# A planned four-block transformer kernel: first loads reordered, small vector operations counted as sharing GpSimd's way, urgencies chosen anew

## The chip, the cores and the metric

The kernel runs on one core of one Trainium2 chip. The metric is the device time of one execution in microseconds, as the median of several runs. The engines are named as the profile names them: PE multiplies matrices, PEld loads its weights, DVE is the vector engine, ACT the scalar engine, POOL is GpSimd, and SP issues most of the loads.

## The reference

Eight sequences of 128 tokens, 256 features wide, pass through four blocks in float32. Each block attends over the same context (also 8 x 128 x 256) and has an MLP with 1024 hidden features.

```python
x = L0(x, ctx)     # layer norm; 16-head cross attention, boolean key mask; gelu MLP
x = L1(ctx, x)     # the latents attend over [context; latents], interleaved k/v weights, integer key mask; RMS norm; MLP
x = L2(x, ctx)     # two cross attentions, 16 heads of 128 features (2048 wide), one learned key and value each; MLP with exact gelu
x = L3(x, ctx)     # self attention with a given score mask, cross attention with another, tanh-gelu MLP
```

Every attention is `softmax(q k^T * scale, masked) v`, followed by an output product and the residual. The time goes into the wide attentions of L2, where q, k and v are 256 by 2048 products.

## The kernel before

The eight sequences are cut into five threads of 1, 1, 2, 2 and 2 sequences (`SIZES`). A thread runs all blocks in order, and the threads overlap: at most three are in the front blocks at once, three in the wide attentions (`FRONTS`, `WIDES`). The last thread's last block is split by sequence (`BY_BATCH`), and some keys and values of L2 are made ahead of time (`AHEAD`).

No order is written by hand. Each piece of work is a Python generator that asks for an operation on an engine. The class `Plan` runs these generators against a planned clock: when an engine is free in the plan, `_choose` takes the asked operation with the lowest urgency; asking for an activation table that is not loaded adds 2.5 to it on ACT. The operation is then issued, so that the instruction order of every engine is what the plan decided. Operations written as `either(...)` go to whichever of ACT and DVE comes to them first. The urgencies are the numbers in `U` (by kind of work) and `LATE` (added for each thread and stage).

How long an operation takes in the plan comes from `_weight`, which also says whether a DVE operation shares its way to SBUF with POOL. If it does, `_end` starts it in the plan at POOL's end, and lets POOL start only after it. In the version before, DVE operations on at most eight elements per partition are never shared:

```python
if n <= 8:
    return 68 + 55 * max(0, len(aps) - 2) * (name == "tensor_scalar"), False
```

A norm's reciprocal square root (`root`) is one planned operation made of ten such small instructions on tiles `rv`, `ry`, `rz`. `dma` plans when a load lands, from a running end `dma_until`; a load marked `early` may also be issued from ACT's queue. If PE has nothing to do in the plan and its planned clock would fall, `idle_work` puts in a filler, a matmul `ident` by `ident` whose result nobody reads. Two PSUM banks serve products (`mm`), two serve transposes and small results (`tl`), four serve scores (`sc`).

All operations pass through one helper, `Engine.call`, and so stand under one line, L335, in the profile. They are told apart by their tiles: `mm<-hT,w` is a projection, `tl<-ident,t` a transpose of softmax weights, `kb<-mm` an eviction, `t<-sc,mask` a masked score, `mx` and `sm` a maximum and a sum of the softmax. In the instruction orders each tile has a number of its own.

Of the kernel before, what the change touches and what calls it, by code (L numbers as in the profile page):

```python
# [18 lines left out]
P = 128  # L19
# [43 lines left out]
FRONTS, WIDES = 3, 3  # L63
BY_BATCH = (4,)
AHEAD = [[(1, 0), (1, 1)], [], [(1, 0)], [], []]
U = {'take': 0.75, 'taken': -1, 'norm': 1.33, 'mask': 5.29, 'k': 2.24, 'q': 0.77, 'v': 3.01, 'by key': 0.17, 'softmax': 1.71, 'weights': 1.17, 'pairs': 0.21, 'out': 0.57, 'mlp norm': -0.18, 'mlp 1': 2.92, 'mlp 2': 3.41, 'wide norm': 1.02, 'wide k': 3.4, 'wide q': 3.13, 'wide v': 5.44, 'wide s': 4.05, 'wide': 0.43, 'ahead': 3.67, 'load': -0.56, 'early': 0.98}
LATE = [(4.59, -1, -1, -0.66, 1.03, -1, 2.77, 3.05, 3.1, 3.0, 2.25, 1.84, 0.92), (16.8, 0.32, 4.0, 6.02, 1.18, -1, 3.37, 3.57, 8.14, 4.15, -0.94, 0.09, 0.94), (2.67, 10.11, 4.03, 1.81, 2.31, 3.16, 3.3, 3.73, 4.79, 13.74, 3.59, 9.93, 9.83), (4.81, 12.33, 4.01, -1, -0.06, 1.37, 3.1, -0.03, 1.5, 1.56, 0.96, -0.5, -1), (1.56, 2.64, -0.58, -0.46, 1.42, -0.16, 4.41, 1.29, 0.75, -1, -1, 3.81, -0.53)]


class Event:  # L70
# [14 lines left out]
class Plan:  # L85
# [12 lines left out]
    def __init__(self):  # L98
        self.now = 0
        self.seq = 0  # L100
        self.events = []
        self.asked = []
        self.until = {e: 0 for e in self.SEEN}
        self.weight, self.shared, self.wrote = 0, False, []
        self.idle_work = None
        self.both_until = {"DVE": 0, "POOL": 0}
        self.clock = Clock()
        self.count = 0
        self.log = []
        self.table = None  # L110
        self.dma_until = 2500
        self.live = {}

    def spawn(self, gen, urgency, after=0):
        end = Event()
        self.live[id(gen)] = gen
        self._later(self.now + after, (gen, urgency, end), None)
        return end
# [146 lines left out]
def _weight(eng, name, args, kw):  # L265

    aps = [x for x in (*args, *kw.values()) if isinstance(x, bass.AP)]
    sizes = [x.free_size() for x in aps]
    n = max(sizes)
    if name == "dma_start":  # L270
        return 480, False
    by_part = sum(m == 1 for m in sizes[1:]) if n > 2 else max(0, len(aps) - 2) if name == "tensor_scalar" else 0
    on_sbuf = all(x.space == bass.MemoryType.SB for x in aps)
    if eng == "PE":
        if name == "transpose":
            return 109, False
        lhsT = kw["lhsT"]
        cols = aps[0].free_size()
        if lhsT.shape[0] < P:
            return 0.539 * cols, False  # L280
        if lhsT.free_size() < P:
            return 0.494 * cols, False
        return max(225, 1.7 * cols), False
    if eng == "ACT":
        if "accum_out" in kw:
            return 385, False
        if name == "copy":
            return 61 + 0.824 * n, False
        return 127 + 0.805 * n + (35 if on_sbuf and n == 256 else 0) + (40 if isinstance(kw.get("bias"), bass.AP) else 0) + (
            90 if isinstance(kw.get("scale"), bass.AP) else 0), False  # L290
    if eng == "DVE":
        if name == "tensor_scalar" and n == 4 and len(aps) == 2 and len(args) > 5:
            return 145, False
        if name == "reciprocal":
            return 65 + 6.25 * n, False
        if name in ("bn_stats", "bn_aggr"):
            return (330 if name == "bn_stats" else 150), False
        if n <= 8:
            return 68 + 55 * max(0, len(aps) - 2) * (name == "tensor_scalar"), False
        if name in ("tensor_scalar", "tensor_copy") and on_sbuf:  # L300
            return 75 + 0.8 * n + 55 * by_part, True
        two = name in ("tensor_tensor", "scalar_tensor_tensor") and sum(
            x.space == bass.MemoryType.SB and x.free_size() > 1 for x in aps[1:]) == 2
        return 72 + 1.03 * n + 55 * by_part, two
    if name == "memset":
        return 20 + n, False
    if n <= 16:
        return 195 + 75 * by_part, False
    if name == "tensor_tensor":
        inner = any(x.ap[-1][0] == 0 for x in aps[1:])  # L310
        return 100 + (1.85 if inner else 2.3) * n, False
    return (150 + 3.0 * n, 10 + 3.6 * n, 5 * n - 20)[by_part], False
# [44 lines left out]
def four_blocks(ctx: ExitStack, tc: tile.TileContext, a: dict, out: bass.AP):  # L357
# [5 lines left out]
    plan = Plan()  # L363
# [73 lines left out]
    def dma(f, kb_, early):  # L437

        def sync():
            f(nc.sync)  # L440
            plan.weight += max(0, plan.dma_until - plan.now - 3500)

        yield op("SP", sync) + (op("ACT", lambda: f(nc.scalar)) if early else ())
        plan.dma_until = max(plan.dma_until, plan.now) + kb_ * 2.8
        yield plan.dma_until - plan.now + 2300

    def load(dst, src, kb_, early=False):
# [189 lines left out]
    def norm(T, src, e, w, b, adds, rows, hT, ready, row_done, urgency):  # L637
# [4 lines left out]
        else:  # L642
# [48 lines left out]
                    nc.vector.tensor_scalar(xn[:, i, :], src[:, i, :], y[:, i, :], z[:, i, :], ALU.mult, ALU.add)  # L691

            yield from each(*(either(lambda i=i: scaled_act(i), lambda i=i: scaled_dve(i)) for i in range(nb)))
        spawn(add_rows(adds, rows, row_done, nb), urgency)
        yield (tl, 1)
        pt = bank("tl")[:, : NC * T.nt].rearrange("p (c b k) -> p c b k", c=NC, b=nb)

# [3 lines left out]
                    nc.tensor.transpose(pt[:, c, i, :], xn[:, i, c * P : (c + 1) * P], ident)  # L701

        yield op("PE", transposes)

        def out_act(c):
            to, s = hT[:, c, :], pt[:, c].rearrange("p b k -> p (b k)")
# [21 lines left out]
    def add_rows(adds, rows, row_done, nb):  # L728
        for (dst, src, _), (r, e) in zip(adds, rows):
            yield e  # L730
            yield op("POOL", lambda: nc.gpsimd.tensor_tensor(
                dst, src, r.unsqueeze(1).to_broadcast([P, nb, D]), ALU.add))
            plan.put(row_slots)
        plan.set(row_done)
# [73 lines left out]
    def key_bias(mask, dst, hs, ks, ks_in, name, dtype, T, may_be_none):  # L808

        nb = T.nb
        raw = mask[:, 0].bitcast(dtype)[:, :, :P]
        m = mask[:, 1]
        ms = new(act, [P, 2, nb], "ms", bufs=4)
        kss = new(act, [P, 2, NC, nb], "kss", bufs=4)
        yield spawn(load(raw, a[name][:, T.tokens].rearrange("o (b k) -> o b k", k=P).partition_broadcast(P), 64 * nb), -1)
        some = new(act, [P, nb], "some", bufs=4)

        def minus():
            nc.vector.tensor_scalar(m, raw, 0.0, -BIG, ALU.is_equal, ALU.mult)
            if may_be_none:
                nc.vector.tensor_reduce(some, m, AX.X, ALU.max)
                nc.vector.tensor_scalar(some, some, -1.0, None, ALU.is_ge)
            else:
                nc.vector.memset(some, 1.0)
            for e in range(2):
                nc.vector.tensor_scalar(hs[:, e], some, half[e], None, ALU.mult)
                nc.vector.tensor_scalar(ms[:, e], some, mask_row[e], None, ALU.mult)  # L830

        def biases():
            for e in range(2):
                for c in range(NC):
                    nc.vector.tensor_scalar(kss[:, e, c], some, ks[:, e, c : c + 1], None, ALU.mult)

        yield op("DVE", minus)
        yield ks_in
        yield op("DVE", biases)
        yield from each(*(  # L840
            op("ACT", lambda e=e, c=c, b=b: nc.scalar.activation(
                dst[:, e, c, b, 0, :], m[:, b], AF.Identity, bias=kss[:, e, c, b : b + 1], scale=ms[:, e, b : b + 1]))
            + op("POOL", lambda e=e, c=c, b=b: nc.gpsimd.tensor_scalar(
                dst[:, e, c, b, 0, :], m[:, b], ms[:, e, b : b + 1], kss[:, e, c, b : b + 1], ALU.mult, ALU.add))
            for e in range(2) for c in range(NC) for b in range(nb)))
# [646 lines left out]
    def inputs():  # L1492
        for T in threads:
            h = T.h
            early = h < 2
            rows = (load(T.x, a["x"][T.batches].rearrange("b p d -> p b d"), 128 * T.nb, early),
                    load(T.ctx, a["ctxT"].rearrange("(c p) t -> p c t", p=P)[:, :, T.tokens], 128 * T.nb, early))
            for f, then in zip(rows, (T.ready, ctx_in[h])):
                spawn(all_then([spawn(f, -3)], then), 0)
            if h == 0:  # L1500
                spawn(all_then([spawn(load(cols, a["cols"], 140, True), -3)], cols_in), 0)
                first = new(const, [P, 1], "first")
                spawn(asks(op("ACT", lambda: nc.scalar.activation(first, ident[:, :1], AF.Exp), None, EXP)), 9)
            spawn(blocks(T), 0)
            yield 4000 if h == 0 else 8000
# [46 lines left out]
```

## Time and profile before

| what | value |
|---|---|
| median of 3 runs | 1195.21 us (1195.16 to 1196.08) |
| the profiled execution | 1194.78 us |
| its span | 1193.0 us |
| mean granted PE clock | 0.993 of full |
| busy: PE, PEld, DVE, ACT, POOL | 1150.5, 956.5, 798.8, 596.3, 360.4 us |
| loaded from HBM | 178.5 MB |

The span runs from the first to the last instruction; the execution has 1.8 us around it. A float32 matmul appears as two PE records, a transpose as one. Their ends are modelled, so PE's busy time is not the time that it needs; the distance from one start to the next shows its pace.

### The profile page before, as it was taken

The page shows a single profiled execution, that of the slowest core. Times are in us where ns is not written, and L with a number is a line of the kernel's source. Part 1 is how long each engine was busy: PE and PEld are TensorE (multiplying, and loading weights), DVE is VectorE, ACT ScalarE, POOL GpSimd, SP SyncE. Part 2 cuts the span into 40 slices and gives each one's busy share as a digit, 9 for nine tenths or more (in the row PEclk, how much of TensorE's full clock was granted, in tenths as well). Part 3 has the DMA queues.
Part 4 walks back from the last instruction along what each step waited for, and adds up shares of the span by engine and source line. Part 5 has one row for each costly group of instructions (what it writes and reads, how often), then busy time and mean ns, then how long its engine had stood idle before and what let it go on. Part 6 is the DMA issues. An engine that isn't in the chain of part 4 may idle for free.

```text
span 1193.0 us, 23579 instructions
## 1 busy us (share of the span) xinstructions
PE 1150.5 (96%) x8816; PEld 956.5 (80%) x8816; DVE 798.8 (67%) x2186; ACT 596.3 (50%) x1538; POOL 360.4 (30%) x446
## 2 busy tenths in 40 slices
PE   7999999999999999999999999999999999988978
PEld 6677788888888878887887878888787778877767
DVE  6867568747776586787477265556855657678972
ACT  3555455355445374557353343633553336367872
POOL 2211211223124253013202022412532226165770
PEclk8999999999999999999999999999999999998999
DMA  9754567787645554435334534446443564351120
GB/s 299 219 162 136 160 201 214 238 273 229 190 143 196 152 185 145 135 112 147 117 116 141 165 106 145 124 131 187 138 137 122 139 183 133 117 143 55 32 85 19
DMA packets 134706, 181.09 MB, mean 152 GB/s; under 512 B 8896, under 2 KB 83392, under 8 KB 134592
## 3 DMA queue, kind: packets, MB, share of 16 engines
q1 hardware_dynamic: 133344, 178.55, 48.7%
q8 instruction: 70, 1.15, 0.4%
q10 hardware_dynamic: 1248, 1.03, 0.3%
q14 instruction: 44, 0.36, 0.1%
HBM read 178.50 MB, written 1.05 MB: 151 GB/s over the span
## 4 chain that ended last, share of the span: by engine, by line
PE 79%; DVE 11%; ACT 5%; DMA 2%; issue 1%; POOL 0%; SPq 0%; ACTq 0%; POOLq 0%; DVEq 0%
PE mm L335 57%; PE tl L335 17%; PE sc L335 5%; DVE rz L335 2%; ACT kb L335 1%; DVE t L335 1%; DMA w<-in_L_wk 1%; DMA bb<-in_L_bias_v 1%; ACT t L335 1%; DVE mn L335 1%; ACT q L335 1%; DVE ry L335 1%; ACT pt L335 1%; DVE kb L335 1%; DVE q L335 1%
## 5 line engine op out<-in xcount | busy, mean ns | idle before, releaser
L335 PE MATMUL mm<-hT,w 128*128 128x256 f32 (+1 forms) x1576 | 292.4, 335 | 12.0 <-ACT kb L335 2.5
L335 PEld LDWEIGHTS mm<-hT,w 128*128 128x128 f32 x1576 | 242.8, 191 | 43.5 <-issue 8.0
L335 POOL TENSOR_TENSOR t<-t,sm 128x512 f32<-128x512 f32 x128 | 132.0, 1041 | 298.5 <-DVE sm L335 242.8
L335 PE MATMUL mm<-ctxT,w 128*128 128x256 f32 (+1 forms) x768 | 148.7, 342 | 1.7 <-DVE x L335 0.8
L335 PE MATMUL mm<-w,ctxT 128*128 128x512 f32 (+1 forms) x352 | 145.9, 542 | 4.6 <-DMA w<-in_L_v_w 2.0
L335 PEld LDWEIGHTS mm<-ctxT,w 128*128 128x128 f32 x768 | 121.7, 194 | 16.5 <-issue 3.0
L335 PE MATMUL mm<-w,at 128*128 128x256 f32 x512 | 121.5, 380 | 0.2 <-DVE kb L335 0.2
L335 PE MATMUL mm<-w,kb 128*128 128x256 f32 x512 | 119.6, 382 | 0.9 <-PE mm L335 0.8
L335 POOL TENSOR_TENSOR x<-x,row 128x256 f32<-128x256 f32 (+1 forms) x48 | 48.0, 999 | 232.7 <-ACT xn L335 108.3
L335 PEld LDWEIGHTS mm<-w,at 128*128 128x128 f32 x512 | 94.7, 190 | 16.2 <-issue 2.6
L335 ACT ACTIVATE t<-t,mn 128x128 f32<-128x128 f32 x256 | 99.5, 395 | 12.8 <-DVE mn L335 11.6
L335 PEld LDWEIGHTS mm<-w,kb 128*128 128x128 f32 x512 | 94.1, 190 | 14.6 <-PE mm L335 1.4
L335 DVE TENSOR_TENSOR x<-mm,x 128x256 f32<-128x256 f32 (+1 forms) x102 | 47.6, 466 | 82.8 <-PE mm L335 82.1
L335 POOL TENSOR_TENSOR t<-t,mask 128x512 f32<-128x512 f32 x64 | 80.2, 1276 | 63.9 <-DVE t L335 62.5
L335 PEld LDWEIGHTS mm<-w,ctxT 128*128 128x128 f32 x352 | 63.0, 192 | 42.7 <-issue 33.6
L335 POOL TENSOR_TENSOR bv<-bv,bb 128x512 f32<-128x512 f32 x40 | 50.8, 1271 | 153.2 <-DMA bb<-in_L_bias_v 137.0
L335 ACT ACT_TABLE_LOAD x60 | 77.0, 1283 | 15.5 <-PE sc L335 6.7
L335 ACT ACTIVATE at<-tl,cols 128x128 f32<-128x128 f32 x212 | 60.4, 371 | 46.5 <-PE tl L335 46.2
L335 PE MATMUL tl<-ident,t 128*128 128x128 f32 x512 | 75.5, 276 | 7.7 <-ACT pt L335 4.4
L335 ACT ACTIVATE kb<-mm,cols 128x256 f32<-128x256 f32 (+1 forms) x168 | 59.5, 422 | 43.5 <-PE mm L335 43.2
L335 PEld LDWEIGHTS tl<-ident,t 128*128 128x128 f32 x512 | 60.0, 141 | 26.0 <-issue 11.6
L335 ACT ACTIVATE t<-t 128x516 f32<-128x516 f32 x64 | 40.4, 634 | 78.4 <-DVE t L335 78.4
(124 smaller groups left out, 1851.7 us busy)
## 6 DMA issues: line engine op xcount, KB each, us to landing
w<-in_L_wk SPq DMA_DIRECT2D x40, 512.0 KB, 4.7
w<-in_L_wv SPq DMA_DIRECT2D x40, 512.0 KB, 4.1
w<-in_L_wq SPq DMA_DIRECT2D x40, 512.0 KB, 4.5
w<-in_L_wo SPq DMA_DIRECT2D x40, 512.0 KB, 4.5
bv<-in_L_bv SPq DMA_DIRECT2D x40, 256.0 KB, 4.7
bb<-in_L_bias_v SPq DMA_DIRECT2D x40, 256.0 KB, 5.7
w<-in_L_mlp_w SPq DMA_DIRECT2D x20, 512.0 KB, 4.8
w<-in_L_w_fc SPq DMA_DIRECT2D x20, 512.0 KB, 4.4
```

The costliest lines, as they stand in the source:

```text
L335: return f(*args, **kw)
```

## The change

It does five things. In the order of the diff: the urgencies in `U` and `LATE` have new values, and the planned end of the first loads is 3300 instead of 2500 ns. Small DVE operations whose operands all lie in SBUF count as shared with POOL in the plan. A load's planned time per KB is 2.9 instead of 2.8 ns. Where a norm is only a transpose (`w is None`), the residual's bias rows are added after the transposes instead of before. And among the first loads the key masks of the first two threads may go over ACT's queue and are more urgent than anything but the bias columns (`cols`), which share their urgency; `x` and the context follow.

```diff
-U = {'take': 0.75, 'taken': -1, 'norm': 1.33, 'mask': 5.29, ..., 'mlp norm': -0.18, ..., 'wide norm': 1.02, ..., 'load': -0.56, 'early': 0.98}
+U = {'take': 0.15, 'taken': -0.55, 'norm': 1.33, 'mask': 5.71, ..., 'mlp norm': -1, ..., 'wide norm': 0.2, ..., 'load': 0.2, 'early': 1.82}
-LATE = [(4.59, -1, -1, -0.66, 1.03, ...
+LATE = [(4.8, 1.85, -1, 2.6, 0.57, ...
...
-        self.dma_until = 2500
+        self.dma_until = 3300
...
         if n <= 8:
-            return 68 + 55 * max(0, len(aps) - 2) * (name == "tensor_scalar"), False
+            return 68 + 55 * max(0, len(aps) - 2) * (name == "tensor_scalar"), on_sbuf and name != "memset"
...
-        plan.dma_until = max(plan.dma_until, plan.now) + kb_ * 2.8
+        plan.dma_until = max(plan.dma_until, plan.now) + kb_ * 2.9
...
-        spawn(add_rows(adds, rows, row_done, nb), urgency)
+        if w is not None:
+            spawn(add_rows(adds, rows, row_done, nb), urgency)
...
         yield op("PE", transposes)
+        if w is None:
+            spawn(add_rows(adds, rows, row_done, nb), urgency)
...
-        yield spawn(load(raw, a[name][:, T.tokens]..., 64 * nb), -1)
+        yield spawn(load(raw, a[name][:, T.tokens]..., 64 * nb, T.h < 2), -5 if T.h < 2 else -1)
...
-                spawn(all_then([spawn(f, -3)], then), 0)
+                spawn(all_then([spawn(f, -4 if early else -3)], then), 0)
...
-                spawn(all_then([spawn(load(cols, a["cols"], 140, True), -3)], cols_in), 0)
+                spawn(all_then([spawn(load(cols, a["cols"], 140, True), -5)], cols_in), 0)
```

More of the change, by code (lines that the diff above doesn't have):

```diff
@@ L65 @@
 AHEAD = [[(1, 0), (1, 1)], [], [(1, 0)], [], []]
-U = {'take': 0.75, 'taken': -1, 'norm': 1.33, 'mask': 5.29, 'k': 2.24, 'q': 0.77, 'v': 3.01, 'by key': 0.17, 'softmax': 1.71, 'weights': 1.17, 'pairs': 0.21, 'out': 0.57, 'mlp norm': -0.18, 'mlp 1': 2.92, 'mlp 2': 3.41, 'wide norm': 1.02, 'wide k': 3.4, 'wide q': 3.13, 'wide v': 5.44, 'wide s': 4.05, 'wide': 0.43, 'ahead': 3.67, 'load': -0.56, 'early': 0.98}
-LATE = [(4.59, -1, -1, -0.66, 1.03, -1, 2.77, 3.05, 3.1, 3.0, 2.25, 1.84, 0.92), (16.8, 0.32, 4.0, 6.02, 1.18, -1, 3.37, 3.57, 8.14, 4.15, -0.94, 0.09, 0.94), (2.67, 10.11, 4.03, 1.81, 2.31, 3.16, 3.3, 3.73, 4.79, 13.74, 3.59, 9.93, 9.83), (4.81, 12.33, 4.01, -1, -0.06, 1.37, 3.1, -0.03, 1.5, 1.56, 0.96, -0.5, -1), (1.56, 2.64, -0.58, -0.46, 1.42, -0.16, 4.41, 1.29, 0.75, -1, -1, 3.81, -0.53)]
+U = {'take': 0.15, 'taken': -0.55, 'norm': 1.33, 'mask': 5.71, 'k': 2.24, 'q': 0.51, 'v': 3.01, 'by key': 0.17, 'softmax': 1.71, 'weights': 1.17, 'pairs': 0.21, 'out': 0.57, 'mlp norm': -1, 'mlp 1': 2.92, 'mlp 2': 3.41, 'wide norm': 0.2, 'wide k': 3.4, 'wide q': 3.13, 'wide v': 5.44, 'wide s': 4.05, 'wide': 0.6, 'ahead': 3.42, 'load': 0.2, 'early': 1.82}
+LATE = [(4.8, 1.85, -1, 2.6, 0.57, -0.78, 2.77, 3.05, 3.1, 4.26, 0.92, 1.84, 0.92), (16.51, 0.4, 2.46, 6.11, 1.1, -1, 4.59, 3.57, 7.89, 3.63, -0.44, -1, -1), (2.67, 13.1, 4.03, 1.89, 2.39, 4.21, 4.35, 3.73, 4.79, 13.55, 3.59, 12.53, 12.43), (4.81, 10.83, 3.75, 0.32, -0.11, 1.32, 3.1, -0.03, 1.86, 1.75, 2.89, -1, 0.1), (2.69, 2.78, -0.58, -0.46, 1.42, -0.16, 3.55, 2.84, -0.29, -1, -1, 3.81, 0.54)]
 class Event:
@@ L817, in key_bias @@
         kss = new(act, [P, 2, NC, nb], "kss", bufs=4)
-        yield spawn(load(raw, a[name][:, T.tokens].rearrange("o (b k) -> o b k", k=P).partition_broadcast(P), 64 * nb), -1)
+        yield spawn(load(raw, a[name][:, T.tokens].rearrange("o (b k) -> o b k", k=P).partition_broadcast(P), 64 * nb, T.h < 2), -5 if T.h < 2 else -1)
         some = new(act, [P, nb], "some", bufs=4)
```

## The prediction

> **What bounds the kernel now.** I read the page first: span, busy times, granted clock, chain of waits.
>
> ```profile
> span 1193.0 us, 23579 instructions
> PE 1150.5 (96%) x8816; PEld 956.5 (80%) x8816; DVE 798.8 (67%) x2186; ACT 596.3 (50%) x1538; POOL 360.4 (30%) x446
> ...
> PEclk8999999999999999999999999999999999998999
> ...
> PE 79%; DVE 11%; ACT 5%; DMA 2%; issue 1%; POOL 0%; SPq 0%; ACTq 0%; POOLq 0%; DVEq 0%
> ```
>
> PE is busy 96% and carries 79% of the chain, so the time is PE work plus the places where PE runs thin. Busy is not peak, so I set a pace: in the timeline's PE rows 24 matmuls of 256 columns take 1046.90 - 1041.72 = 5.18 us, 0.216 us each.
>
> ```profile
> 1041.72 5.34 PE L335 MATMUL mm<-hT,w 128*128 128x256 f32 x24
> 1046.90 0.60 PE L335 MATMUL tl<-ident,xn 128*128 128x128 f32 x4
> ```
>
> The closest spacings of the other forms are 0.43 (512 columns), 0.111 (128) and 0.034 us (four-row-block forms). Records times spacing, fillers left out, give 1097.3 us of PE work; 1193.0 - 1097.3 = 95.7 us are lost. Placed by time: 34.9 us in 0 to 150, 27.4 in 150 to 1050, 33.4 in 1050 to 1193. The busy times of those stretches say which engine is near its limit:
>
> ```profile
> 0.00:150.00 150.00, 134.23 (x1290) 110.39 (x1291) 104.87 (x344) 71.30 (x141) 34.22 (x73) 0.97 0.63 195
> 150.00:1050.00 900.00, 891.35 (x6421) 741.86 (x6421) 591.92 (x1560) 431.25 (x1052) 243.76 (x286) 1.00 0.52 159
> 1050.00:1193.00 143.00, 124.88 (x1109) 104.25 (x1107) 101.99 (x283) 93.75 (x346) 82.37 (x87) 0.98 0.21 61
> ```
>
> Columns: PE, PEld, DVE, ACT, POOL. The long middle is PE at 99% and can hardly get better; a reordering wins or loses at the two ends. The tail's worst stall in the timeline, all engines:
>
> ```profile
> 1071.69 1.27 POOL L335 TENSOR_TENSOR t<-t,mask 128x512 f32<-128x512 f32 x1
> 1071.75 1.22 DVE L335 TENSOR_TENSOR rz<-ry 128x1 f32<-128x1 f32 x1
> ...
> 1072.91 2.04 POOL L335 TENSOR_TENSOR t<-t,sm 128x512 f32<-128x512 f32 x2
> ...
> 1073.01 0.96 DVE L335 TENSOR_TENSOR rz<-rz,rv 128x1 f32<-128x1 f32 x1
> ...
> 1074.01 0.96 DVE L335 SCALAR_TENSOR_TENSOR ry<-rz,ry 128x1 f32<-128x1 f32 x1
> ...
> 1075.91 0.69 DVE L335 COPY pt<-tl 128x512 f32<-128x512 f32 x1
> ...
> 1076.66 0.58 PE L335 MATMUL tl<-ident 128*128 128x128 f32 x1 [3.94 <-DVE pt L335]
> ```
>
> Three one-element DVE steps of a root, 0.16 us elsewhere, take 1.22, 0.96 and 0.96 and end with the POOL instructions beside them. The eviction `pt` queues behind the root, PE waits 3.94 us, and the clock records show half speed from 1075.6 to 1082.4. The planner before did not know of this wait. Over the whole trace 54 DVE operations are over 0.1 us longer than their usual form, 32.0 us together, 10.4 of them in 1050 to 1150.
>
> **The change part by part.** The instruction orders of the two programs give what moves; work is the same but for the choice of engine.
>
> *Planner's sharing rule.* Small all-SBUF DVE operations now wait in the plan for POOL's end, and POOL waits for the whole DVE operation that holds one. Here a rule of the Trainium skill speaks against part of it. Row first:
>
> ```profile
> L335 DVE TENSOR_SCALAR t<-mx 128x4 f32<-128x4 f32 x64 | 17.5, 280 | 1.0
> ...
> L335 DVE TENSOR_TENSOR rz<-ry 128x1 f32<-128x1 f32 x48 | 11.5, 240 | 1.7
> ...
> L335 DVE TENSOR_SCALAR rv<-mv 128x1 f32<-128x1 f32 x22 | 3.4, 154 | 0.8
> ```
>
> Splitting records by whether a POOL instruction over 0.6 us ran meanwhile: `t<-mx` 167 ns alone and 546 beside POOL, `rz<-ry` 163 and 533, but `rv<-mv` 128x1 154 and 154 (8 beside POOL). "SBUF — State Buffer", section "Who interferes with whom", says that a DVE instruction with two SBUF inputs contends with a POOL instruction that reads SBUF, while one with at most one SBUF input, outside the two-port modes, does not. The rows agree: the change counts the one-input 128x1 forms as blocked although they are not, and it holds POOL back over a whole root (ten instructions, about 2 us) where POOL in the trace started amid it at 1072.91. By the change's own count the plan fits the chip, its extra fillers stand in real gaps, and they cost 0. By the rule some planned waits do not exist, and fillers put there would delay PE: 24 more (60 against 36), two 0.11 us records each, at most 5.3 us. I take +1: most of the rule's cases agree with the change.
>
> *The stall at 1064 to 1085.* In both orders the last matmul of thread 4's third MLP leaves 95.9 us of PE work. Before, it ends at 1064.0 and the first score of the last block follows at 1085.4: 21.4 us in which 11.1 us of PE work stand. After, 17.6 us stand there, 6.5 more, for the same DVE and ACT chain (norm, transposes, q, k), and 5 fillers instead of 2. If the chain takes as long, 6.5 us are won; below 0 if the added matmuls hold the chain's PSUM banks. I take -5, half-speed stretch included.
>
> *Where that work is taken from.* Thread 2's last MLP (16 matmuls of 256 columns, 6.9 us) then no longer covers the second batch's norm. Before, from that batch's output product (1120.35) to its next transposes (1127.90) 7.5 us pass, with 6.3 us of work inside, its own 0.9 counted; after, 2.4 us. Bare for up to 5.2 us; the fillers there number 14. DVE is the busier engine in that stretch and has less before it in the new order, so I take +3.5 (ends 0 and 5.2).
>
> *Locks elsewhere that reach PE.* A second root is blocked at 1147.92 and 1148.99 (1.04 and 0.97 us), ahead of a 3.64 us PE wait at 1152.45; others cost under 1 us. An order that knows them avoids some: -2 (ends 0 and -4).
>
> *The start.* `cols` goes from second to first on ACT's queue, `mask` from fourth to first on SP's, `x` to ACT's second; the first key weight goes from SP's second to ACT's third place, the value weight the other way; thread 1's context moves to SP, its mask to ACT. Two rows are traded:
>
> ```profile
> 6.64 1.32 PE L335 MATMUL mm<-ctxT,w 128*128 128x128 f32 x8
> ...
> 9.61 0.23 DVE L335 TENSOR_SCALAR mask<-mask 128x128 f32<-128x128 uint8 x1 [3.15 <-DMA mask<-in_mask_b]
> ...
> 9.92 1.39 PE L335 MATMUL mm<-w,ctxT 128*128 128x256 f32 x4 [1.96 <-DMA w<-in_L_v_w]
> ...
> 20.37 1.22 PE L335 MATMUL sc<-k,q 32*128 32x128 f32 x32
> ```
>
> The third load on ACT landed at 9.8, so the key product moves from 6.6 to about 9.8, and the value product follows at once instead of waiting: both are done near 11.3 as now. The mask arrives some 6 us sooner, but ACT reaches the key biases only behind two DMA issues that stand until 11.7 as before (each load waits for the eighth before it). First score near 20: -1 (ends -4 and +3).
>
> *ACT.* Table loads rise from 60 to 78, 18 x 1.283 = 23.1 us; moved evictions add about 14 us by their rows, DVE loses 17.
>
> ```profile
> L335 ACT ACT_TABLE_LOAD x60 | 77.0, 1283 | 15.5 <-PE sc L335 6.7
> ```
>
> In the middle ACT goes from 48% to some 52% busy, and a matmul product of 1.73 us on the other `mm` bank covers one load: 0. Without that cover a load costs up to 1.28. The rest (later start of `dma_until`, 2.9 for 2.8 per KB, `add_rows` asked after the transposes where there is no norm) moves loads in a plan whose PE waits on DMA total under 3 us: 0.
>
> Sum: +1 - 5 + 3.5 - 2 - 1 + 0 = -3.5 us. The profiled execution took 1194.8 (span 1193.0 and 1.8 around it), so 1191.3; the median stands 0.4 above it, so 1191.7, or about 1191.5.
>
> **The rivals.**
>
> *ACT's table loads uncover (slower).* Place: ACT's evictions of `mm` in the middle, where a load now stands before them 18 times more. Price c per load between 0 and 1.28; the two-bank cover leaves nothing over when a second eviction waits too, so c = 0.6: -3.5 + 18 x 0.6 = +7.3, about 1202.5. It decides from c = 0.2 on. For it: a count of PE rows whose eviction has less PE work before it than its own row lasts rises from 95 to 101. Against: PE's own waits on ACT total 14.8 us now (list of waits, PE rows).
>
> *No difference.* The stall at 1064 only moves to the second batch, +5.2 for -5, and the plan's knowledge of locks wins nothing: 1195.
>
> *Both ends win.* Cover at 1064 without the loss later, start -4, locks -4: about 1184.
>
> **How the numbers follow.** My sum 0.36 (1187 to 1192.8), both ends 0.12, no difference 0.18, table loads 0.34. Runs here differ by 0.1%; 0.2%, 2.4 us, is about what can be told from no change. Faster 0.48, same 0.18, slower 0.34. The range leaves out the last tenth of either side: 1181 to 1203. With both signs in it, the likeliest case's own range is 1187 to 1193.
>
> **What would show it.** Right: PE losses in 1050 to the end below 33 us, no half-speed stretch near 1075, the 3.94 us wait gone, 14 fillers in one gap some 15 us before the last scores. Wrong: PE losses in 150 to 1050 above 35 us with evictions behind table loads (the rival), a first score after 22 us, or locked DVE time as high as 32 us.

## Result: slower by 1.2%, lost at both ends

The changed kernel takes 1209.86 us (median of 4 runs, 1208.8 to 1211.07) against 1195.64 for the kernel before on the same chip (1195.16 to 1197.5): ratio 1.0116, 95% interval 1.01 to 1.0133. I had said 1191.5 us, in a range of 1181 to 1203. The page of the profile after:

```profile
span 1208.9 us, 23673 instructions
...
PE 1160.8 (96%) x8864; PEld 966.8 (80%) x8864; DVE 784.0 (65%) x2153; ACT 629.4 (52%) x1576; POOL 360.4 (30%) x447
...
PEclk8999999999999999999999999999999999999999
...
PE 80%; DVE 8%; ACT 7%; DMA 3%; issue 1%; POOL 1%; ACTq 0%; SPq 0%; POOLq 0%; DVEq 0%
```

DVE is 15 us less busy and its share of the chain fell from 11 to 8%, and still the span is 15.9 us longer, so the relief of DVE bought no time. By stage (columns PE, PEld, DVE, ACT, POOL, PE clock):

```profile
0.00:150.00 150.00, 131.92 (x1243) 107.11 (x1244) 96.74 (x312) 77.99 (x143) 31.33 (x67) 0.94 0.61 187
150.00:1050.00 900.00, 885.61 (x6421) 739.02 (x6420) 584.72 (x1543) 449.40 (x1072) 243.65 (x288) 1.00 0.52 158
1050.00:1208.90 158.90, 143.25 (x1204) 120.69 (x1202) 102.58 (x298) 102.03 (x361) 85.44 (x92) 0.98 0.22 66
```

In the first stretch DVE did 96.74 us of work against 104.87 before, in the same 150 us. Fixed stretches mix a delay with what follows it, so the two traces are better compared by PE's work: the time at which PE starts a given amount of it (records times closest spacing, fillers left out, as in the prediction; 1097.3 us in both).

| PE work started, us | before | after | difference |
|---|---|---|---|
| 0 | 6.64 | 8.50 | +1.9 |
| 12 | 28.68 | 32.96 | +4.3 |
| 26 | 43.51 | 53.70 | +10.2 |
| 100 | 132.15 | 141.35 | +9.2 |
| 1000 | 1063.03 | 1074.07 | +11.0 |
| 1034 | 1110.36 | 1115.06 | +4.7 |
| 1066 | 1157.10 | 1173.53 | +16.4 |
| end | 1192.99 | 1208.91 | +15.9 |

Read by rows: 10 us are lost in the first 54 us, nearly nothing (1.8) in the 900 us of the middle, 6.3 are won at the stall of thread 4, and 11.7 are lost again just behind it. PE's rows of the start, from the timeline after:

```profile
8.50 2.05 PE L335 MATMUL mm<-ctxT,w 128*128 128x128 f32 x8 [2.38 <-DMA w<-in_L_k_w]
...
22.23 1.58 PE L335 MATMUL sc<-k,q 32*128 32x128 f32 x32
...
29.25 1.17 PE L335 MATMUL sc<-q,k 32*128 32x128 f32 x32
...
39.21 1.17 PE L335 MATMUL sc<-k,q 32*128 32x128 f32 x32
...
49.12 2.00 PE L335 MATMUL mm<-w,attnT 128*128 128x256 f32 x4 [2.56 <-DVE kss L335]
...
51.48 1.68 PE L335 MATMUL sc<-q,k 32*128 32x128 f32 x32
```

The first score is at 22.23 (before 20.37), but the fourth one, thread 1's second, is at 51.48. Before, the third and the fourth stand here:

```profile
30.34 1.17 PE L335 MATMUL sc<-q,k 32*128 32x128 f32 x32
...
37.43 1.17 PE L335 MATMUL sc<-q,k 32*128 32x128 f32 x32
```

DVE's two largest waits in 5 to 45 us (us in total, times, longest), after and then before:

```profile
DVE st L335 <- DMA x<-in_x: 7.9, 1, 7.9
DVE kb L335 <- ACT kb L335: 5.1, 2, 3.5
```
```profile
DVE hT L335 <- ACT hT L335: 3.5, 2, 2.6
DVE mask L335 <- DMA mask<-in_mask_b: 3.1, 1, 3.1
```

After, DVE's queue stands 7.9 us behind thread 1's `x` and another 3.5 behind one key eviction. In the tail there are the 14 fillers that I had foretold in one gap (16 and 12 records, two each), and 15 more later:

```profile
1137.48 2.67 PE L335 MATMUL mm<-ident 128*128 128x128 f32 x16 [0.62 <-DVE k L335]
1141.18 0.44 PE L335 MATMUL tl<-ident,xn 128*128 128x128 f32 x2 [1.03 <-ACT xn L335]
1141.45 1.70 PE L335 MATMUL mm<-ident 128*128 128x128 f32 x12
...
1158.85 4.21 PE L335 MATMUL mm<-ident 128*128 128x128 f32 x18
...
1163.33 1.70 PE L335 MATMUL mm<-ident 128*128 128x128 f32 x12
```

### The profile page after: what moved, and what is told of

The parts are those of the page before. It is cut to its first block, busy times and chain, and to the rows that moved or that the text cites. A ratio compares the mean times of both kernels' runs of the same rounds, so it can differ in the third digit from the quotient of the medians.

```text
span 1208.9 us, 23673 instructions
## 1 busy us (share of the span) xinstructions
PE 1160.8 (96%) x8864; PEld 966.8 (80%) x8864; DVE 784.0 (65%) x2153; ACT 629.4 (52%) x1576; POOL 360.4 (30%) x447
## 4 chain that ended last, share of the span: by engine, by line
PE 80%; DVE 8%; ACT 7%; DMA 3%; issue 1%; POOL 1%; ACTq 0%; SPq 0%; POOLq 0%; DVEq 0%
PE mm L335 59%; PE tl L335 16%; PE sc L335 5%; ACT t L335 2%; DMA bb<-in_L_bias_v 1%; DVE t L335 1%; DMA w<-in_L_wk 1%; ACT pt L335 1%; ACT q L335 1%; DVE tm L335 1%; DVE rz L335 1%; DVE q L335 1%; ACT kb L335 1%; ACT L335 1%; DMA w<-in_L_k_w 1%
## 5 line engine op out<-in xcount | busy, mean ns | idle before, releaser
L335 PE MATMUL mm<-hT,w 128*128 128x128 f32 (+1 forms) x1576 | 293.8, 335 | 9.8 <-DVE q L335 2.6
L335 POOL TENSOR_TENSOR t<-t,sm 128x512 f32<-128x512 f32 x128 | 132.2, 1040 | 280.0 <-DVE sm L335 194.9
L335 ACT ACTIVATE kb<-mm,sb 128x256 f32<-128x256 f32 (+1 forms) x86 | 35.3, 430 | 83.9 <-PE mm L335 71.6
L335 ACT ACTIVATE at<-tl,cols 128x128 f32<-128x128 f32 x196 | 55.6, 369 | 42.5 <-PE tl L335 42.3
```

The source lines that it names most:

```text
L335: return f(*args, **kw)
```

## How the experiments are made

The planner reacts to every edit by reordering everything behind it, so a version with one edit undone differs everywhere. I therefore recorded the two orders: for each engine the operations one after the other, and for each pool the grants of its buffers. A kernel can replay such a list; an engine then issues only the next operation of its list:

```python
want = self.left[stream][-1] if self.left.get(stream) else None
return ids.index(want) if want in ids else None
```

The arithmetic and all tiles stay as they are. At 80 us and at 1000 us of PE work both orders have issued exactly the same matmuls, so they can be spliced there. Each list below is one edit of `ORDER`. Differences "at work w" are against the kernel before, in one profiled execution of each. The same start differs from one execution to another by 1 us, in one run by 2, and the profiled execution as a whole can lie up to 4 us from the median of its run (s_dma 1202.42 against 1206.15, t_new2 1198.18 against 1194.24). So medians and ratios of timed runs stand beside them, and a ratio is always to the kernel before on the same chip. The marks of the lists are not quite those of the table: the mark 1040 lies at about 1033 in the table's count.

## Which end costs what

**Start alone.**

```diff
-ORDER = before
+ORDER = after until 80 us of work, before from there
```

> The order of the changed kernel (every engine's instructions, fillers, loads, grants of buffers) up to 80 us of matmul work, then the order of the kernel before; at that mark both orders have issued the same matmuls. Theory S (the start costs some 10 us on the chip and nothing later gives it back): 1204 to 1207 us, against 1195.6 for the kernel before. Rival (the late start eats slack that the middle has, or the loss sits in the tail alone): at most 1198 us.

1207.64 us, ratio 1.0107 (1.0091 to 1.0123). +8.3 at work 26, +10.0 at 100, +10.0 at 1000 and +10.0 at the end: the start's loss passes through the middle and the tail unchanged. The rival, that the middle takes the loss up or that it lies in the tail alone, falls.

**Tail alone.**

```diff
+ORDER = before until 1000 us of work, after from there
```

> The order of the kernel before up to 1000 us of matmul work (again a mark at which both orders have issued the same matmuls), then the order of the changed kernel. If start and tail add up (start +10, middle +1, tail +4 to +5): 1200 us. If the tail's loss is only the echo of the late start and of the changed middle (other buffers, other clock windows): 1191 to 1196 us.

1199.09, ratio 1.0034 (1.0021 to 1.0047); +0.6 at work 1000, -6.7 at 1034, +5.4 at 1066, +4.5 at the end. By these executions start (10.0), middle (about 1) and tail (4.5) add up to 15.5 of the 15.9. By the medians start and tail are 12.7 and 4.2, 16.9 together, against 14.2 for the changed kernel, so the close sum of the spans is in part luck.

## The tail: cover that is only moved

**The changed order in the stall alone.**

```diff
+ORDER = before until 1000, after until 1040, before from there
```

> The kernel before, with the changed order only between 1000 and 1040 us of matmul work: thread 2's last MLP fills the stall of thread 4's norm, and three of its four last pieces are gone later; what follows is the order before. Cover theory (the same matmuls can fill one hole or the other): the stall gives back 4 to 6 us and the holes at 1046 to 1066 us of work take 5 to 10: 1196 to 1201 us. Order theory (the later loss comes from the changed order of the last block's own products, not from the missing matmuls): 1190 us.

1200.34, ratio 1.0045 (1.0028 to 1.0061). -5.4 at work 1034, +6.5 at 1066: the stall is filled, and the order before, which is fine where thread 2's pieces still cover it, loses 11.9 us without three of them. The order theory (1190) falls.

**The stall kept.**

```diff
+ORDER = before until 1040, after from there
```

> The kernel before up to 1040 us of matmul work, its stall kept, then the changed order: the last MLP's second product of thread 2 stands later than in the changed kernel, but ahead of the last block's second attention. Cover theory: the cover is still there in part, 1196 to 1200 us. Order theory: the changed order of the last block loses its 10 us here too, 1205 us.

1205.09, ratio 1.0088 (1.0073 to 1.0103); -0.1 at work 1034, +11.2 at 1066. The time is what the order theory said, but no proof of it: this splice issues thread 2's four pieces at 1034 to 1041 us of work (from 1112.4 us on), ahead of the gap, so it has no cover there either. Alone it does not decide between the two.

**The pieces put into the gap.** This asks directly whether the bare gap can be bought back.

```diff
-PE, mm grant, DVE add of thread 2's last product: behind its first product
+the same, and one load on SP: in place of the 14 fillers ahead of the second batch's norm
```

> The run t_ba (before up to 1000 us of work, then the changed order; span 4.5 us over the kernel before) with one product moved: the four pieces of the second product of thread 2's last MLP, 6.9 us of matmuls, stand where the changed order has 14 fillers ahead of the second batch's norm, and the fillers there are left out. If the bare hole is the loss and the pieces are not missed where they came from: 5 us faster than t_ba, 1194. If cover is only moved (the place that they leave opens as wide): 1198 to 1203.

1204.04, ratio 1.0067 (1.0044 to 1.009), against 1.0034 for the tail that it mends: some 4 us slower. The rows where the fillers were:

```profile
1127.78 3.72 PE L540 MATMUL mm<-w,kb 128*128 128x256 f32 x16 [0.65 <-DVE k L540]
1131.48 0.44 PE L540 MATMUL tl<-ident,xn 128*128 128x128 f32 x2
1131.75 3.62 PE L540 MATMUL mm<-w,kb 128*128 128x256 f32 x16
...
1138.69 1.17 PE L540 MATMUL sc<-k,q 32*128 32x128 f32 x32 [2.45 <-DVE t L540]
```

The gap is full and its own loss falls from 5.8 to 1.5 us (work 1048 to 1052), but where the pieces came from the lead of 4.2 us at work 1016 becomes a lag of 3.9 at 1034, and a new DVE wait of 2.45 follows. Cover moved by hand was worth less than in either planner's place.

**Without fillers.**

```diff
-31 fillers behind thread 2's last product
```

> The run t_ba (before up to 1000 us of work, then the changed order) without the 31 fillers that stand behind the last MLP of thread 2 (62 matmul records). My prediction priced fillers at 0 to 5.3 us and took 1. If fillers stand in front of real products: 1 to 4 us faster than t_ba, 1195 to 1198. If they only fill bare stretches: 1199, as t_ba. If they hold the clock up: half-speed stretches of 3.4 us appear and it is 2 to 5 us slower, 1201 to 1204.

1201.25, ratio 1.0051 (1.0034 to 1.0068), against 1.0034 for the same tail with them; the intervals overlap. The profiled span is 0.7 shorter, 1196.8, but the clock records show half speed for 6.8 us from 1128.6 and 10.2 from 1149.1, where the tail with fillers has 3.4. The timed runs agree on the clock: their mean is 0.984 to 0.990 without the fillers and 0.993 to 0.995 with them. A cost of the fillers does not show: one execution is 0.7 us shorter without them, the medians are 2 us longer, and both are within the noise.

**Other tails.** If the planner can be fitted to both sharing rules, it should find a tail as good.

```diff
-LATE, U = before
+ORDER = before until 1000 us of work; then free, with LATE and U searched for a short plan under both rules
```

> The order before up to 1000 us of work, then the tail planned anew with other urgencies, searched for a short tail both with and without the new sharing rule (this one starts from the changed urgencies). If an order fitted to both rules fits the chip: 1193 to 1195, 0 to 2 us faster than before. If the planner's clock cannot tell orders apart at this level: 1196 to 1201 like the other tails.

> As the run t_new1, but searched from the urgencies of the kernel before: the second product of thread 4's third MLP first, thread 2's last MLP behind it. Fitted order: 1192 to 1194. Planner's clock too coarse: 1196 to 1201.

1197.21, ratio 1.0009 (0.9999 to 1.0018), and 1194.24, ratio 0.9992 (0.9979 to 1.0005), both with 12 runs. Both keep the start of the kernel before, so this compares tails alone: the second is equal to the tail before as far as can be told, and nothing tried beats it.

## The start: which edit, and which part of it

**One edit at a time**, up to some 60 us of work, the order before from there:

```diff
+s_loads: cols -5, x -4, mask -5 and early
+s_dma:   dma_until = 3300, kb_ * 2.9
+s_flag:  small all-SBUF operations shared
```

> Up to 58 us of matmul work the order that the planner makes with the new order and urgencies of the first loads alone (old urgencies, old sharing rule, old planned load times), then the order before. Load theory (cols and masks in front, the key weight third on its queue: that is what delays the start): 1202 to 1206 us, most of it in the first 12 us of work. Plan theory (the loads only move the first products by a microsecond or two; the start is lost where the planner believes that loads land later or small operations are blocked): 1195 to 1199 us.

> Up to 56 us of matmul work the order that the planner makes with the new planned load times alone (3300 for 2500 ns, 2.9 for 2.8 ns per KB), then the order before. My prediction priced this edit at 0. Plan theory: loads planned later put the mask operations and what follows them later into DVE's queue, and the start loses 4 to 8 us: 1199 to 1203. Load theory: within 1 us of the kernel before, 1195 to 1196.

> Up to 64 us of matmul work the order that the planner makes with the new sharing rule alone, then the order before. Plan theory: planned waits for GpSimd that the chip does not have reorder DVE's queue, 4 to 7 us lost: 1199 to 1202. Rival (the rule fits the chip, its order is as good): 1194 to 1197.

| run | median, us | ratio | at work 26 | at 100 | end |
|---|---|---|---|---|---|
| s_loads | 1201.86 | 1.0059 (1.0042 to 1.0076) | +2.3 | +5.0 | +6.2 |
| s_dma | 1206.15 | 1.0085 (1.0065 to 1.0106) | +7.6 | +6.9 | +7.7 |
| s_flag | 1201.46 | 1.0055 (1.0037 to 1.0073) | +9.0 | +4.8 | +5.8 |

Neither theory was right: by the spans every edit costs 6 to 8 us alone and all together 10, by the medians 7, 11 and 6 alone and 13 together (s_ab). They do not add. What they have in common is that each makes the planner choose another order in the first 60 us, and the order before was better than all of these. The clearest case is s_flag: it leaves the first 32 loads of SP and all of ACT's early ones as they were, and still costs 6 us. What I called "0" in the prediction, the planned load times, leaves the first five loads of SP and those of ACT alone, moves some later ones, and costs 8 us by the span and 11 by the medians. The new urgencies and the later bias rows were not tried alone.

**Loads against computing order.** All runs so far changed both. These two cross them, up to 80 us of work:

```diff
+l_b: SP's list and the loads in ACT's list from after, all else before
+l_a: SP's list and the loads in ACT's list from before, all else after
```

> The order of the kernel before on PE, DVE, ACT's computing and GpSimd, with the changed kernel's order of loads on both queues up to 80 us of work (cols and masks first, the first key weight third on ACT, thread 1's x and mask on ACT, the x and contexts of threads 2 to 4 ahead of rows and value biases). Load theory (the loads themselves delay the start): 1203 to 1207. Order theory (the loads cost what their later landing costs, the rest is lost by the computing order that the planner made for them): the first product is 1.9 us later, 1196 to 1200.

> The counterpart: the changed kernel's computing order up to 80 us of work with the load order of the kernel before, then the order before. Order theory: the start stays slow, 1202 to 1207. Load theory: 1196 to 1199.

| | loads before | loads after |
|---|---|---|
| computing order before | 0 | +3.5 at work 26; 1197.17, ratio 1.002 (1.001 to 1.003) |
| computing order after | +11.0 at work 26; 1207.02, ratio 1.0101 (1.0084 to 1.0117) | +8.3 at work 26; ratio 1.0107 (run s_ab) |

That settles which half it is. With the old computing order the new loads cost 2 us by the medians and 4 by the spans. The new computing order costs 12 with the old loads, and 6 (spans) to 10 (medians) on top of the new ones. The busy times of the first 40 us (third busy column DVE), of before, l_b, l_a and after in turn, show what it does:

```profile
0.00:40.00 40.00, 32.81 (x295) 28.09 (x296) 27.57 (x113) 17.66 (x37) 13.04 (x35) 0.91 0.81 261
```
```profile
0.00:40.00 40.00, 30.95 (x228) 25.79 (x232) 24.57 (x105) 15.07 (x34) 11.34 (x34) 0.87 0.78 258
```
```profile
0.00:40.00 40.00, 31.36 (x226) 26.74 (x226) 20.39 (x88) 13.37 (x28) 10.02 (x30) 0.83 0.86 277
```
```profile
0.00:40.00 40.00, 31.95 (x253) 26.80 (x257) 21.14 (x92) 14.01 (x30) 9.99 (x30) 0.87 0.86 277
```

The order before keeps DVE busy for 27.6 us, and still 24.6 with the later loads; the changed order for 20 to 21. PE's busy time is alike in all four and tells nothing. ACT has done less too, so DVE's work was not handed to ACT: it is late. But DVE's work is no measure of the loss. In s_flag (first row below) it is 24.50 us, as in l_b, and yet s_flag is 9.0 us behind at work 26 and l_b only 3.5. Nor is it the clock: s_ab (second row) is granted as much as the kernel before, 0.91 up to 40 us and 1.00 from there to 60, and loses its 10 us all the same.

```profile
0.00:40.00 40.00, 29.77 (x254) 24.98 (x254) 24.50 (x102) 12.19 (x25) 12.85 (x33) 0.91 0.79 256
```
```profile
0.00:40.00 40.00, 30.91 (x258) 26.52 (x258) 21.45 (x93) 14.02 (x30) 10.04 (x30) 0.91 0.84 277
```

Then I tried to find the one place in that order, three times in vain.

**A bank.** Thread 2's key product holds one of two `mm` banks until its mask's biases are there.

```diff
-PE: thread 2's first-block key product, then ..., thread 0's output product
+PE: ..., thread 0's output product, then thread 2's key product
```

> The changed order up to 80 us of work, then the order before (as in the run s_ab, whose span was 10.0 us over the kernel before), with one product moved: thread 2's first key product (1.7 us of matmuls) and its grant of an mm bank stand after thread 0's output product instead of some 10 us ahead of it. In the changed order this product is done at 36 us, but its eviction waits for the key biases from the mask until 53 us, so that one of the two mm banks is taken and the output product waits for the four q evictions of the other. Bank theory: 3 to 5 us of the 10 come back, 1200 to 1202 and the loss between 20 and 26 us of work (now 6 us) falls to 1 to 3. Rival (DVE's own queue is the limit there): 1204 or more.

1206.64, ratio 1.0092 (1.0077 to 1.0107); +9.8 at work 26, +11.9 at the end. The bank theory falls.

**Two places of DVE's queue.**

```diff
-DVE: statistics of thread 1's x ahead of thread 0's key evictions
+DVE: behind them
-DVE: statistics and root of thread 2's x behind the first wide key eviction
+DVE: ahead of it
```

> The start of the run s_ab (the changed order up to 80 us of work, then the order before; span 10.0 us over the kernel before) with only DVE's order mended in two places: the statistics of thread 1's x, whose load lands at 15 to 16 us, stand behind thread 0's first key evictions instead of ahead of them, and the statistics and root of thread 2's x, landed since 19 us, stand ahead of the key eviction for which DVE sits idle for 3.5 us instead of behind it. Theory of DVE's queue (in the first 60 us DVE is busy 35.8 us in the changed kernel against 45.3 before: its queue waits behind an operation whose input is late): 4 to 6 of the 10 us come back, 1199 to 1202. Rival (DVE is only the messenger, PSUM banks or the granted clock limit): 1204 or more.

1205.26, ratio 1.0082 (1.0055 to 1.0109). At work 12 it is 1.5 us ahead of s_ab, at 26 the gain is gone. DVE's waits show where it went:

```profile
DVE kb L540 <- ACT kb L540: 7.2, 1, 7.2
DVE mp L540 <- PE sc L540: 3.4, 2, 3.1
```

The mended waits were 6.9 and 3.5 us in s_ab; the idle time came back as 7.2 in front of the next operation and 3.1 in front of a score maximum. My reading, which no run shows: DVE ran out of things to do, since the scores that give it work stand late in PE's list.

**The turn at the score banks.** In the order before thread 1's first scores come ahead of thread 0's second ones; the changed order, s_dma and s_flag have it the other way.

```diff
+if T.h == 0:
+    yield turn        # set when thread 1's first scores have their banks
```

> All five edits, and one constraint in the planner: thread 0's second score product waits until thread 1's first one has had its turn at the four score banks, as it has in the order before (there thread 1's first scores start at 24.9 us and thread 0's second ones at 30.3; in the changed kernel thread 0's come at 29.2 and thread 1's only at 39.2). The order planned so up to 62 us of matmul work, then the order before. Turn theory (losing this turn sets thread 1's attention back by 10 us, and PE has nothing else): the start's 10 us fall to 2 to 5, 1198 to 1201, and the score products come by turns near 30 us. Rival (the turn is one of many small shifts, each later operation of DVE's queue counts): 1203 to 1206.

> The same constraint with the new planned load times as the only edit (the run s_dma without it: span 7.7 us over the kernel before), up to 54 us of work, then the order before. Turn theory: 1196 to 1199. Rival: 1201 to 1205.

1204.02, ratio 1.0063 (1.0043 to 1.0083), and 1205.48, ratio 1.0084 (1.0067 to 1.0102). The turn is back, thread 1's scores come first (timeline of s_turn):

```profile
29.77 1.72 PE L540 MATMUL sc<-k,q 32*128 32x128 f32 x32
...
36.15 1.17 PE L540 MATMUL sc<-q,k 32*128 32x128 f32 x32
```

and 9.8 us are still lost at the end of s_turn and 12.9 of d_turn. The turn theory falls as well. It brought back thread 1's first scores only: its second ones still start at 50.74 in s_turn and 51.62 in d_turn. That start goes with the loss better than DVE's work does: it is at 37.4 to 40.9 us in the kernel before and in the runs that are at most 3.5 us behind at work 26 (s_loads, l_b), and at 46.5 to 52.3 in all the others. No run moves it alone, so it may be a sign and not the cause. What stays open is which few swaps carry the 10 us, if any few do. PE's list of one order cannot be joined with DVE's of the other to find out: thread 1's maxima would wait for scores that wait for the four banks that the maxima release. That was not tried. Shown is that most of the start's loss lies in the computing order of the first 60 us; how it comes about is not.

## Why the prediction was wrong, point by point

- *Start, -1 (-4 to +3)*: the step that failed. I priced the loads, by the rows of two products: the key product did move (to 8.50, for 9.8 foretold), the value product did follow it (11.89). With the computing order held fixed, this costs 2 to 4 us (l_b). But I took the computing order of the start as moved by no more than the loads. The start measured +10.0 by the span and +12.7 by the medians (s_ab), 6 to 10 of it from the computing order. My own sign for it, a first score after 22 us, came at 22.23.
- *Planned load times, 0*: +7.7 alone by the span, 11 by the medians (s_dma). "PE waits on DMA total under 3 us" was no argument: the number acts through the order that the planner makes.
- *Sharing rule, +1*: a cost of the fillers does not show (t_nofill), so +1 for them is neither confirmed nor refuted. The reordering was put at nothing: +5.8 in the start alone (s_flag). Reading the rule of the Trainium skill ("SBUF — State Buffer", section "Who interferes with whom") against single rows could not tell that.
- *Locks elsewhere, -2*: DVE operations over 0.1 us longer than their form fell from 54, 32.0 us, to 42, 24.6 us. The sign came true, but no run shows PE time for it. Row of one of the blocked forms, before 240 ns:

```profile
L335 DVE TENSOR_TENSOR rz<-ry 128x1 f32<-128x1 f32 x48 | 9.3, 193 | 1.7
```

- *The stall, -5*: right. -7.3 between work 1000 and 1034 in t_ba, -6.3 in the changed kernel. PE's longest wait for DVE's `pt` in the tail is 1.0 us instead of 3.94; half-speed stretches of 3.4 us remain at 1083.4 and come at 1168.7.

```profile
PE tl L335 <- DVE pt L335: 1.2, 2, 1.0
```

- *Where the work is taken from, +3.5 (0 to 5.2)*: right in mechanism, a third of its size. The gap with the 14 fillers alone costs 5.8 (t_ba, work 1048 to 1052), and the stretch from 1034 to 1066 costs 12.1. I bounded the loss by the one gap that I saw, at 5.2, and it passed that bound alone; the other 6.3 us are lost on both sides of it, where I had priced nothing.
- *Table loads in the middle, 0, and the rival built on them*: 78 loads are there, and the middle (work 100 to 1000) costs 1.8 us, not 10.8. PE's losses in 150 to 1050 are 31.4 us by the same count, under the 35 that I had set as the mark. The rival named the right sign for a wrong reason.

```profile
L335 ACT ACT_TABLE_LOAD x78 | 100.1, 1283 | 23.0 <-PE sc L335 12.8 <-PE mm L335 3.6 <-DVE mn L335 2.8
```

- *Signs*: PE losses in 1050 to the end were to be below 33; they are 38.1.

The sum again with the measured terms, from the profiled spans: start +10.0, middle +1 to +2, stall -7.3, gaps behind it +12.1, end of the tail -0.8: some 15.5 us.

## What to carry to other kernels

Where a planner decides the order, price an edit of its inputs by the order that comes out, not by the edit: the sharing rule alone, which moved none of the first loads, cost half as much as the whole start. Read the two orders engine by engine from the first instruction, and ask of each engine how much it has done by 20 and 40 us, and when each thread's first products start; an engine that falls behind early is not seen in PE's busy share. And a covering product can be spent once: before counting a filled stall as won, list every wait, not only the largest, that it covered where it stood.

## What the runs showed of the hardware that I had not expected

Splitting four evictions of one product between ACT and DVE gave no overlap. The changed kernel's four `q` evictions of thread 2 (timelines of ACT and of DVE), and the same four on ACT alone in the kernel before:

```profile
46.66 0.56 ACT L335 ACTIVATE q<-mm,qs,par 128x256 f32<-128x256 f32 x1 [1.09 <-PE mm L335]
47.83 0.56 ACT L335 ACTIVATE q<-mm,qs,par 128x256 f32<-128x256 f32 x1 [0.61 <-DVE q L335]
```
```profile
47.26 0.54 DVE L335 TENSOR_SCALAR q<-mm,par,qs 128x256 f32<-128x256 f32 x1 [0.90 <-ACT q L335]
48.43 0.54 DVE L335 TENSOR_SCALAR q<-mm,par,qs 128x256 f32<-128x256 f32 x1 [0.63 <-ACT q L335]
```
```profile
40.62 1.94 ACT L335 ACTIVATE q<-mm,qs,par 128x256 f32<-128x256 f32 x4
```

Each one waits for the one before it on the other engine, so the two engines take 2.31 us for what one does in 1.94. Why they wait so is not shown. A one-input DVE operation on 128x2 elements, `rv<-mv`, took 170 ns alone and 449 in the mean when a GpSimd instruction over 0.6 us ran beside it in the trace before, while the 128x1 form took 154 in both cases. And without 31 fillers PE was granted half speed for 17.0 us of the tail instead of 3.4 (t_nofill against t_ba), with no change in time beyond the noise.
